# Two attention layers and two MLPs on one core: the value products of a key tile for all 512 queries in one group, behind the second pair's scores

## The chip, the cores and the metric

One core of one Trainium2 chip runs the whole kernel. The time is the device time of one execution in microseconds; the median of three executions is compared. The profile is of one further execution, taken by the hardware profiler. PE is the matrix engine (its weight loads are a row of their own, PEld), ACT the scalar engine, DVE the vector engine, POOL the general one, SP the engine that issues most DMAs. PE writes its results to PSUM, from where ACT and DVE read them.

## The reference

The input x has 2048 rows of 256 numbers, all in float32. Four layers follow each other:

```python
x = x + attn_a(layernorm(x))   # 16 query heads, 4 key/value heads, head size 16, rotary, biases
x = x + ffn(layernorm(x))      # 256 -> 2048 -> 256, gated tanh-gelu, 4-bit weights to be unpacked
x = x + attn_b(layernorm(x))   # 16 heads of 16, no rotary, no biases
x = x + ffn(layernorm(x))
```

Both attentions are causal over all 2048 positions:

```python
scores = einsum("bthd,bshd->bhts", q, k) * scale
scores = where(tril, scores, -inf)
attended = einsum("bhts,bshd->bthd", softmax(scores), v)
```

## The kernel before

The queries are cut into 4 blocks of 512 (b), the 16 heads into 4 groups of four (g). A unit is one (b, g): four heads and 512 queries against all keys up to the block's end, in 4(b+1) key tiles of 128. Each attention has 16 units, one after the other; `run` (L950) lists their steps, and `weave` (L43) puts the steps of one unit and side work into the one order in which every engine's queue is filled. The order is written by the program and kept: each engine takes its instructions in it.

A unit needs the row maxima first. They are found one unit ahead: `max_steps` (L752) multiplies queries by keys with queries on the partitions (L763, two heads at once in the two halves of the rows), and DVE reduces each result over the keys (L775). `gather` and `turn` bring the maxima into a form from which PE itself subtracts them.

`value_steps` (L824) does the unit proper. A key tile takes two steps, one for each pair of heads. `pair(kt, p)` (L852) writes a pair's scores with keys on the partitions: two small matmuls put the negative maxima in (L860), two add the scores (L865), and ACT takes the exponentials into a tile e in SBUF (L877). `values` (L829) then multiplies the exponentials of the key tile before by its values (L845): four matmuls, one a head, into four strips of 32 partitions of one PSUM tile ps_av, which is summed over all key tiles of the unit. A matmul of float32 numbers stands twice in the trace, so four matmuls are eight records. A column of ones beside the values gives the sums of the exponentials. `end` copies ps_av out, and `divide` turns it and divides. On the last four key tiles of a unit (the diagonal) only part of the queries is left: 512, 384, 256 and 128 of them, and triangular masks are added by further small matmuls (L738).

The scores of `pair` and of `max_steps` go to the same PSUM tiles: ps_s (L122) has three buffers of two banks each, used in turn. A buffer is free again when ACT has taken its exponentials, or DVE its maxima. The e tiles have four buffers, ps_av and ps_m one each.

In an ordinary place the order on PE is thus: scores of the first pair, a block of scores for the next unit's maxima, value products; scores of the second pair, another block for the maxima, value products. `values(0)` behind the first pair does the first 256 of 512 queries for all four heads, `values(1)` behind the second pair the other 256. A key tile with 256 queries or fewer is done whole behind the first pair; one with 384 in parts of 128 and 256. Only the last unit of each attention (b = 3, g = 3), which has no next unit and so no maxima beside it, does every key tile whole, behind the second pair. Beside the steps of a unit run further side steps: the projections of the next block of queries (`prep_steps`), the output projection of the block before (`out_steps`), and in the first attention the unpacking of the 4-bit weights.

`class Mlp` (L1018) then runs the feed-forward layer on the same ps_s, ps_m and ps_av buffers.

Of the kernel before, what the change touches and what calls it, by code (L numbers as in the profile page):

```python
# [27 lines left out]
NG = NH // 4  # L28
MLP = 2048
NFC = MLP // P  # L30
TB = 512
NB = S // TB
# [48 lines left out]
def tile_hybrid_layers(  # L81
# [40 lines left out]
    def ps_s():  # L122
        return psum.tile([P, 2, 512], F32, tag="s", name="ps_s", bufs=3)

    def ps_av():
        return psum.tile([P, 512], F32, tag="av", name="ps_av")

    def ps_m():
        return psum.tile([P, 512], F32, tag="m", name="ps_m")
# [281 lines left out]
    class Attention:  # L411
# [412 lines left out]
        def value_steps(self, b, g):  # L824

            nk = NT * (b + 1)
            held = {"pending": []}

            def values(half):  # L829


                self.settle()
                kt, q0, es_ = held["pending"][0]
                whole = (b, g) == (NB - 1, NG - 1)
                few = whole or TB - q0 <= TB // 2
                if half == 1:
                    held["pending"].pop(0)
                if few and half != whole:
                    return
                if kt == 0 and half == whole:  # L840
                    held["av"] = ps_av()
                own = slice(q0, TB) if few else slice(*((q0, TB // 2), (TB // 2, TB))[half])
                for j in range(4):
                    h = g if self.first else 4 * g + j
                    nc.tensor.matmul(  # L845
                        held["av"][32 * j : 32 * j + 32, own],
                        lhsT=self.vv[kt // NT][:, kt % NT, h * VW : h * VW + 32],
                        rhs=es_[j // 2][:, j % 2, own],
                        start=(kt == 0 and half == whole), stop=(kt == nk - 1),
                    )  # L850

            def pair(kt, p):  # L852
                q0 = max(0, kt - NT * b) * P
                diagonal = kt >= NT * b
                keys = slice((kt % NT) * P, (kt % NT + 1) * P)
                self.settle()
                pt = ps_s()

                for r in range(2):
                    nc.tensor.matmul(  # L860
                        pt[:, r, q0:], lhsT=sel[64 * r : 64 * r + 64, p, :],
                        rhs=self.mT[b, g][64 * r : 64 * r + 64, q0:], start=True, stop=False,
                    )
                for r in range(2):
                    nc.tensor.matmul(  # L865
                        pt[:, r, q0:], lhsT=self.key_rows(kt // NT, g, p, r, keys),
                        rhs=self.qT[b, g][64 * r : 64 * r + 64, p, q0:],
                        start=False, stop=not diagonal,
                    )
                e = self.wk.tile([P, 2, TB], F32, tag="e", name="e", bufs=4)  # L870

                def masked():
                    self.add_mask(pt, 1, q0)
                    exponentials()

                def exponentials():
                    nc.scalar.activation(e[:, :, q0:], pt[:, :, q0:], AF.Exp, scale=QK_SCALE)  # L877

                if diagonal:
                    self.owed.append(("exp", masked))  # L880
                else:
                    exponentials()
                if p == 0:
                    held["es"] = [e]
                else:
                    held["pending"].append((kt, q0, held["es"] + [e]))

            def end():
                values(0)
                values(1)  # L890
                o = pre.tile([P, TB], F32, tag="o", name="o")
                nc.scalar.copy(o, held["av"])
                held["o"] = o

            def divide():
                o = held["o"]
                pt = ps_m()
                for i in range(NT):
                    nc.tensor.transpose(
                        pt[:, i * P : (i + 1) * P], o[:, i * P : (i + 1) * P], ident  # L900
                    )
                heads = pt.rearrange("p (t j c) -> p t j c", t=NT, c=32)
                rec = small.tile([P, NT, 4], F32, tag="rec", name="rec")
                nc.vector.reciprocal(rec, heads[:, :, :, HD])
                if g == 0:
                    self.att[b] = pre.tile([P, NT, NG, 4, HD], F32, tag="att", name="att")
                nc.vector.tensor_tensor(
                    self.att[b][:, :, g], heads[:, :, :, :HD],
                    rec.unsqueeze(3).broadcast_to([P, NT, 4, HD]), ALU.mult,
                )  # L910

            steps = []
            for kt in range(nk):
                for p in range(2):
                    scored = lambda kt=kt, p=p: pair(kt, p)
                    steps.append((scored, lambda p=p: values(p)) if kt else scored)
            return steps, end, divide
# [295 lines left out]
```

## Time and profile before

| | |
|---|---|
| median of 3 runs | 1848.21 us (1847.87 to 1849.67) |
| the profiled execution | 1858.67 us |
| its span, first to last instruction | 1856.9 us |
| granted PE clock, mean | 0.987 |
| PE busy | 1775.3 us, 96% |
| DVE busy | 1127.8 us, 61% |
| ACT busy | 802.9 us, 43% |
| first attention, first pair of the first unit to first pair of the last | 46.9 to 583.4 us |
| second attention, the same | 976.2 to 1480.2 us |
| a unit of the last block (second attention, g = 1 and 2) | 46.4 and 46.3 us |

In the groups of the profile a row gives the line, the engine, the operation, the tile written and the tiles read, the shape and the count, then busy time, the mean of one in ns and the idle time ahead of it. In the timeline the first number is the start in us, the second the length; x8 is eight records that lie together, and a bracket gives the idle time of that engine just before and whose end closed it. PE's matmuls are pipelined and their ends are modelled, so the distance from one start to the next is what a group of matmuls really takes.

### The profile page before, as it was taken

The numbers are of one execution on the slowest core, as the hardware profiler recorded it, in microseconds if no ns is written. First come the engines' busy times: TensorE is split into PE (matmuls) and PEld (weight loads), VectorE is DVE, ScalarE is ACT, GpSimd is POOL, SyncE is SP. The second block draws the span as 40 slices with busy tenths as digits, with TensorE's granted clock in tenths as the row PEclk, the third lists the DMA queues.
The fourth block names the chain that finished last, engine by engine and source line by source line (L and its number), as shares of the span: only waits on it lengthen the run. The fifth ranks groups of instructions, "written<-read, shape, count | busy, mean of one in ns | idle before, by whom it ended". The sixth has DMA issues, their size and how long they took to land. (4 is left out here: it accounts for less than half of the span.)

```text
span 1856.9 us, 31581 instructions
## 1 busy us (share of the span) xinstructions
PE 1775.3 (96%) x13342; PEld 923.2 (50%) x13342; DVE 1127.8 (61%) x1679; ACT 802.9 (43%) x1071; POOL 240.2 (13%) x444
## 2 busy tenths in 40 slices
PE   9889989999999999999998998999999999999999
PEld 4444444444443465747464444444444434655656
DVE  4567778788785544363545677767877726354442
ACT  1335455556667422132314354565666663132221
POOL 4031201120012211012101010000000001011110
PEclk7799999999999999999999999999999999999999
DMA  5131300120000200003203314014000010000000
GB/s 137 49 75 44 74 31 24 32 61 19 24 13 30 91 6 1 1 1 74 51 0 77 62 49 79 13 46 72 22 12 2 1 46 1 12 3 9 7 6 12
DMA packets 41887, 63.43 MB, mean 34 GB/s; under 512 B 13713, under 2 KB 20753, under 8 KB 41489
## 3 DMA queue, kind: packets, MB, share of 16 engines
q1 hardware_dynamic: 33104, 45.41, 8.4%
q0 software_dynamic: 7680, 15.48, 5.0%
q8 instruction: 105, 1.72, 0.4%
q10 hardware_dynamic: 960, 0.52, 0.1%
q14 instruction: 38, 0.30, 0.1%
HBM read 43.45 MB, written 17.83 MB: 33 GB/s over the span
## 5 line engine op out<-in xcount | busy, mean ns | idle before, releaser
L775 DVE TENSOR_REDUCE mx<-ps_s 128x2 f32<-128x1024 f32 (+3 forms) x640 | 660.6, 1061 | 224.9 <-PE ps_s L738 114.9
L877 ACT ACTIVATE e<-ps_s 128x1024 f32<-128x1024 f32 (+3 forms) x640 | 568.8, 898 | 401.9 <-PE ps_s L865 229.7
L845 PE MATMUL ps_av<-e,v 128*32 128x256 f32 (+2 forms) x4384 | 351.5, 392 | 0.0
L865 PE MATMUL ps_s<-qT,kT 64*128 64x512 f32 (+3 forms) x1280 | 336.4, 523 | 0.0
L763 PE MATMUL ps_s<-kT,qT 64*128 64x512 f32 (+3 forms) x1280 | 269.7, 422 | 29.8 <-ACT e L877 13.5
L860 PE MATMUL ps_s<-mT,sel 64*128 64x512 bf16 (+3 forms) x1280 | 231.2, 355 | 25.0 <-ACT mT L817 10.7
L1062 PE MATMUL ps_s<-xnT,wg 128*128 128x512 f32 x512 | 240.9, 593 | 0.0
L1062 PE MATMUL ps_s<-xnT,wu 128*128 128x512 f32 x512 | 240.6, 592 | 0.0
L860 PEld LDWEIGHTS <-sel 64*128 64x128 bf16 x1280 | 75.1, 93 | 252.5 <-issue 243.1
L763 PEld LDWEIGHTS ps_s<-kT,qT 64*128 64x128 f32 x1280 | 129.0, 187 | 140.3 <-ACT e L877 65.3
L1068 ACT ACTIVATE t<-ps_s 128x512 f32<-128x512 f32 x128 | 76.3, 596 | 243.8 <-PE ps_s L1062 243.6
L1071 ACT ACTIVATE t<-t 128x512 f32<-128x512 f32 x128 | 80.5, 629 | 199.2 <-DVE t L1070 199.2
L1070 DVE TENSOR_TENSOR t<-ps_s,t 128x512 f32<-128x512 f32 x128 | 88.1, 689 | 123.5 <-POOL t L1069 121.5
L1062 PEld LDWEIGHTS ps_s<-xnT,wu 128*128 128x128 f32 x512 | 97.3, 190 | 122.5 <-issue 122.5
L1069 POOL TENSOR_SCALAR t<-t 128x512 f32<-128x512 f32 x128 | 79.4, 620 | 533.8 <-ACT t L1068 530.3
L1062 PEld LDWEIGHTS ps_s<-xnT,wg 128*128 128x128 f32 x512 | 95.1, 190 | 104.2 <-issue 102.5
L1072 DVE SCALAR_TENSOR_TENSOR t<-t,ps_s 128x512 f32<-128x512 f32 x128 | 88.2, 689 | 89.0 <-ACT t L1071 89.0
L845 PEld LDWEIGHTS ps_av<-e,v 128*32 128x32 f32 x4384 | 87.2, 108 | 94.3 <-issue 79.9
L865 PEld LDWEIGHTS ps_s<-qT,kT 64*128 64x128 f32 x1280 | 129.2, 197 | 0.0
L1087 PE MATMUL ps_m<-wd,inter 128*128 128x256 f32 x512 | 114.5, 380 | 0.0
L1087 PE MATMUL ps_av<-wd,inter 128*128 128x256 f32 x512 | 114.5, 380 | 0.0
L1087 PEld LDWEIGHTS ps_av<-wd,inter 128*128 128x128 f32 x512 | 96.7, 190 | 17.1 <-issue 4.5
(147 smaller groups left out, 1221.6 us busy)
## 6 DMA issues: line engine op xcount, KB each, us to landing
qT<-h SPq DMA_DIRECT2D x248, 64.0 KB, 2.2
kT<-h POOLq DMA_DIRECT2D x88, 128.0 KB, 5.4
h<-high SPq DMA_DIRECT2D x24, 256.0 KB, 2.1
h<-low SPq DMA_DIRECT2D x24, 256.0 KB, 2.2
wd<-wd_kept SPq DMA_DIRECT2D x2, 2048.0 KB, 7.8
wd_kept<-dq_d SPq DMA_DIRECT2D x4, 512.0 KB, 2.7
out<-x SPq DMA_DIRECT2D x16, 128.0 KB, 1.7
x<-x SPq DMA_DIRECT2D x3, 512.0 KB, 7.6
```

The source lines that it names most:

```text
L763: nc.tensor.matmul(pt[:, r, :w], lhsT=self.qT[b, g][64 * r : 64 * r + 64, p, i * P : (i + 1) * P], rhs=self.key_rows(c, g, p, r, slice(0, w)),
L775: nc.vector.tensor_reduce(held["mx"][:, i, 2 * p : 2 * p + 2, c], pt[:, :, :w], AX.X, ALU.max)
L845: nc.tensor.matmul(held["av"][32 * j : 32 * j + 32, own], lhsT=self.vv[kt // NT][:, kt % NT, h * VW : h * VW + 32], rhs=es_[j // 2][:, j % ...
L860: nc.tensor.matmul(pt[:, r, q0:], lhsT=sel[64 * r : 64 * r + 64, p, :], rhs=self.mT[b, g][64 * r : 64 * r + 64, q0:], start=True, stop=False,)
L865: nc.tensor.matmul(pt[:, r, q0:], lhsT=self.key_rows(kt // NT, g, p, r, keys), rhs=self.qT[b, g][64 * r : 64 * r + 64, p, q0:], start=Fals ...
L877: nc.scalar.activation(e[:, :, q0:], pt[:, :, q0:], AF.Exp, scale=QK_SCALE)
L1062: nc.tensor.matmul(pt[:, k, :], lhsT=w[:, c, fc * P : (fc + 1) * P], rhs=self.xnT[b][:, c, :], start=(c == 0), stop=(c == 1),)
L1069: nc.gpsimd.tensor_scalar(t, t, GELU_A, 1.0, ALU.mult, ALU.add)
L1070: nc.vector.tensor_tensor(t, gate, t, ALU.mult)
L1071: nc.scalar.activation(t, t, AF.Tanh, scale=GELU_C)
L1072: nc.vector.scalar_tensor_tensor(t, t, 1.0, gate, ALU.add, ALU.mult)
L1087: nc.tensor.matmul(po[:, :D], lhsT=inter[:, fc, i * P : (i + 1) * P], rhs=wd[:, fc, :], start=(fc == 0), stop=(fc == NFC - 1),)
```

## The change

The two halves of `values` become one. Behind the first pair of a key tile nothing is done but what is owed for the masks; behind the second pair the four matmuls are issued for all queries that are left of the key tile before, up to 512. The two special cases, the last unit and the tiles of 256 queries or fewer, fall away, since all units now follow one rule. The line numbers behind the change are four lower: L845 becomes L841, L860 L856, L865 L861, L877 L873.

```diff
             def values(half):
 
-
                 self.settle()
                 kt, q0, es_ = held["pending"][0]
-                whole = (b, g) == (NB - 1, NG - 1)
-                few = whole or TB - q0 <= TB // 2
-                if half == 1:
-                    held["pending"].pop(0)
-                if few and half != whole:
+                if half == 0:
                     return
-                if kt == 0 and half == whole:
+                held["pending"].pop(0)
+                if kt == 0:
                     held["av"] = ps_av()
-                own = slice(q0, TB) if few else slice(*((q0, TB // 2), (TB // 2, TB))[half])
+                own = slice(q0, TB)
                 for j in range(4):
                     h = g if self.first else 4 * g + j
                     nc.tensor.matmul(
                         held["av"][32 * j : 32 * j + 32, own],
                         lhsT=self.vv[kt // NT][:, kt % NT, h * VW : h * VW + 32],
                         rhs=es_[j // 2][:, j % 2, own],
-                        start=(kt == 0 and half == whole), stop=(kt == nk - 1),
+                        start=(kt == 0), stop=(kt == nk - 1),
                     )
```

## The prediction

> **What bounds the kernel now.** I read the page's engine shares first, then its costliest groups, then the waits, and last the timeline of single steps. I write S for the two mask and two score matmuls of one pair (L860, L865), M for one score block of the next unit's maxima (L763), V for a group of value products (L845). S and M each take one of three buffers of ps_s; ACT frees that of an S (exponential, L877), DVE that of an M (reduction, L775).
>
> ```profile
> PE 1775.3 (96%) x13342; PEld 923.2 (50%) x13342; DVE 1127.8 (61%) x1679; ACT 802.9 (43%) x1071; POOL 240.2 (13%) x444
> ...
> L845 PE MATMUL ps_av<-e,v 128*32 128x256 f32 (+2 forms) x4384 | 351.5, 392 | 0.0
> ```
>
> PE is busy nearly all the time, so what shortens PE's work shortens the kernel, as long as PE doesn't wait instead. Who makes it wait is in the waits:
>
> ```profile
> PEld ps_s L763 <- ACT e L877: 65.3, 178, 1.5
> PEld ps_s L763 <- DVE mx L775: 44.6, 113, 1.4
> ```
>
> M is what waits, mostly for ACT: for the buffer of an earlier S. One ordinary step of a late unit (second attention, third block of keys complete) shows how near this lies:
>
> ```profile
> 1395.48 0.39 PE L860 MATMUL ps_s<-mT,sel 64*128 64x512 bf16 x2
> ...
> 1396.20 1.02 ACT L877 ACTIVATE e<-ps_s 128x1024 f32<-128x1024 f32 x1 [0.48 <-PE ps_s L865]
> ...
> 1396.83 0.39 PE L860 MATMUL ps_s<-mT,sel 64*128 64x512 bf16 x2
> ...
> 1397.28 0.19 PEld L763 LDWEIGHTS ps_s<-kT,qT 64*128 64x128 f32 x2 [0.24 <-ACT e L877]
> 1397.29 0.49 PE L763 MATMUL ps_s<-kT,qT 64*128 64x512 f32 x2
> ...
> 1397.71 0.64 PE L845 MATMUL ps_av<-e,v 128*32 128x256 f32 x8
> 1398.28 0.39 PE L860 MATMUL ps_s<-mT,sel 64*128 64x512 bf16 x2
> ```
>
> From start to start: S 0.46, M 0.42, V 0.57, a step of 1.45 us, two of them for a key tile. The order is S M V S M V. With three buffers, the M at 1397.29 takes the buffer of the S at 1395.48, three uses back. That S's exponential starts 0.72 later, lasts 1.02 and ends at 1397.22; M starts 0.07 behind it. So an M follows the S three uses before it by at least 0.72 + 1.02 + 0.06 = 1.80 us. Today S, M, V, S lie between the two, 1.91 us of PE work: the wait is just covered, and V is what covers it.
>
> Where V is missing, the wait is open. At the start of a unit there is no key tile whose values could be taken yet:
>
> ```profile
> 1388.70 0.39 PE L860 MATMUL ps_s<-mT,sel 64*128 64x512 bf16 x2
> ...
> 1389.20 0.50 PE L763 MATMUL ps_s<-kT,qT 64*128 64x512 f32 x2
> ...
> 1389.72 0.39 PE L860 MATMUL ps_s<-mT,sel 64*128 64x512 bf16 x2
> ...
> 1390.60 0.19 PEld L763 LDWEIGHTS ps_s<-kT,qT 64*128 64x128 f32 x2 [0.67 <-ACT e L877]
> 1390.60 0.49 PE L763 MATMUL ps_s<-kT,qT 64*128 64x512 f32 x2 [0.25 <-ACT e L877]
> ```
>
> S M S M: the second M starts 0.88 us behind its S where 0.42 to 0.46 is usual, 1.90 behind the first S. (ACT was also held some 0.1 by the copy of o.) In the 22 units that start so, with two or more blocks of keys, this distance lies between 1.89 and 2.22.
>
> **What the change does, and its terms.** By the instruction order of the two kernels, 198 key tiles lose their two V of 256 queries for one of 512, behind the second M; 30 lose a V of 128 and one of 256 for one of 384. The last unit of each attention has this form already, and the narrower diagonal tiles only move by one step. No other engine's order changes.
>
> Term 1, the merged V. The last unit shows the form:
>
> ```profile
> 1493.05 0.10 PEld L860 LDWEIGHTS <-sel 64*128 64x128 bf16 x2 [0.26 <-issue]
> 1493.06 0.39 PE L860 MATMUL ps_s<-mT,sel 64*128 64x512 bf16 x2
> ...
> 1493.60 1.07 PE L845 MATMUL ps_av<-e,v 128*32 128x512 f32 x8
> 1494.60 0.39 PE L860 MATMUL ps_s<-mT,sel 64*128 64x512 bf16 x2
> ```
>
> 1.00 from V to the next S, against 2 x 0.57 = 1.14: 0.14 saved. The two V of 384 there take 0.78, against 0.57 + 0.36 = 0.93: 0.15 saved. In all 198 x 0.14 + 30 x 0.15 = 32 us less for PE. A rule would make this smaller: the Trainium skill, "TensorE: Matmul & The Clock Gate", Part 2, Back-to-back issue gap, puts a warm matmul at its columns over 2.4 GHz plus 2.5 ns. By that eight records fewer save 20 ns a key tile, 228 x 0.02 = 5 us. The rows show a fixed part of 0.14 for a group of eight records in four column strips (0.57 for 256 columns, 1.00 for 512), and I take the rows: 32.
>
> Term 2, the wait that V covered. The order becomes S M S M V. Start the first S at 0. M follows at 0.46, the second S at 0.87, and PE reaches the second M at 1.33. It needs the first S's buffer, which is free at 1.80: a stall of 0.47. V stands behind that M in PE's order, so it can't fill the gap, though its exponentials have long been there; behind V stand all later scores. Then M 0.34 (as short as it is after a wait) and V 1.00: the next S starts at 3.14. That S takes the first M's buffer: reduction from 0.46 + 0.54 = 1.00 to 2.23 (0.54 and 1.23 by the rows at 1390.60 and 1391.14 of the same timeline), so it has no wait. Period 3.14.
>
> I sorted the 198 periods (first S of a key tile to the first S of the next) of the trace by what lies in them:
>
> - 49 full-width with two M and nothing else: now 2.92 on average, then 3.14: +0.22, +10.8 us.
> - 51 full-width with three M. S M M S M V: the second S needs the first S's buffer, 1.80; the third M the first M's, 2.28; V at 2.62, next S at 3.62. S M S M M V ends at 3.6 too. Three reductions of 1.23 are 3.69. I take 3.65 against 3.42 now: +11.7 us.
> - 7 with four M: four reductions are 4.9 us, DVE sets them before (4.3 with narrow blocks among them) and after: 0.
> - 19 on the first diagonal tile without other work: the S of 384 queries, its masks and an exponential of 0.81 free the buffer at 1.95, and ten periods of 3.17 become 1.95 + 0.28 + 0.23 + 1.00 = 3.46; the other nine like them. About +0.25 each: +4.7 us.
> - 72 in which PE does something else too (projections, transposes, 0.6 to 2 us). In 53 it lies ahead of the fourth buffer use and covers the wait; 19 still have it, 10.4 us together. Against that, 72 x 0.14 = 10.1: 0.
> - the 30 tiles of 384: their pairs have few M beside them, no new wait: -4.5 us.
>
> Sum: 10.8 + 11.7 + 4.7 + 0 - 4.5 = +22.7 us. In other words, stalls of 82 us (the same count by distance alone, 145 tiles at 0.57), of which 27 take the place of waits that PE has today (2.92 and 3.42 are more than the bare work; DVE's backlog, too, is worked off in the stall), less 32.
>
> Moves at no price: the V of 256 queries on the third diagonal tile goes from behind the first S to behind the second; no M lies there, its exponentials are over, cost between 0 and 0.1 for 30 tiles, I take 0. The e buffers (four): V still ends before the S whose exponential reuses them, 0.72 ahead; no new wait. The accumulation stays in the one ps_av; its first V comes one step later, by which the copy of o of the unit before is long done. The gated clock: PE's new gaps are half a microsecond, like those that it has at each unit start, where the clock row stays at 9 of 10; 0.
>
> The profiled execution took 1858.67 us (span 1856.9 and 1.8 around it), 10.5 above the median of the runs, 1848.21. The sum is 1.2% of either: a profiled execution near 1881, a median of 1871.
>
> **Rivals.** (A) Slower by about 23 us, as above: chance 0.73, +8 to +42. For it: the wait can be read at every unit start, and PE's order is fixed.
> (B) Faster: the merged V pays and the buffer wait hardly adds. The skill speaks for it: "Perfetto Trace Analysis", Optimizing Tensor Performance, Matmuls, says "Larger matmuls are more efficient than smaller matmuls, when possible." By that alone the sum is term 1, -32 us, 1816. The trace agrees about the V and disagrees about its surroundings; the same section wants groups to rotate through banks so that evacuation overlaps, and three buffers are what runs out here. Mechanism: the new stalls merely replace PE waits of today. It decides where new stalls net of vanished ones come below 32 us, 0.22 a tile on 145 tiles; I find 82 - 27 = 55, 0.38 a tile. Chance 0.11, 1816 to 1844.
> (C) Nothing given back: all 82 us of stall stand, PE's other waits remain: 82 - 32 = +50, 1898. For it: at unit starts the stall comes on top of the rest. Chance 0.13.
> (D) The two terms cancel within 0.2% (3.7 us, about what measurement can tell from no change): 0.03.
>
> **How the numbers follow.** The likeliest is A, 1871. B is below 1848, C is near 1898; a range from 1855 to 1899 holds A and most of C, and leaves out B and D and a tail of C, less than 2 in 10. A alone gives 1856 to 1890. Faster 0.11, within 0.2% 0.04, slower 0.85.
>
> **What would show it.** Right: V groups of eight records at 1.00 from V to S; the wait of M's weight loads on ACT's e rising from 65 us to over 110; in late units a period of 3.1 to 3.2 with the second M about 0.8 to 0.9 behind its S, where now 0.42 is usual; units two and three of the last block (46 us) up by about 3 us. The MLP stretches and the last unit of each attention unchanged. Wrong: a second M that starts at its usual 0.42 behind S (an exponential that frees its buffer earlier than 1.80), or V costing other than 1.00 beside M; or DVE's waits shrinking so much that periods with three M don't grow.

## The result and the profile after

| | before | after |
|---|---|---|
| median | 1848.86 us (1847.87 to 1849.67, 4 runs) | 1880.95 us (1879.07 to 1883.33, 4 runs) |
| ratio | | 1.0165 (95%: 1.0136 to 1.0193) |
| profiled execution, span | 1858.67, 1856.9 us | 1880.94, 1879.2 us |

The change makes the kernel 32 us slower. In the profiles the two attentions take 15.2 and 13.7 us longer between the points that were measured before (40.2 to 591.9 and 984.7 to 1502.4 now), and what lies between and behind these stretches is the same. That the two profiled spans differ by 22 only has its reason ahead of them: in the profile before, the first pair starts at 46.9, in the profiles of all other kernels here between 38.4 and 42.8.

On the page of the kernel after, PE's shares and the group of the value products:

```profile
PE 1725.9 (92%) x11518; PEld 872.0 (46%) x11518; DVE 1128.8 (60%) x1679; ACT 794.7 (42%) x1071; POOL 239.9 (13%) x444
...
L841 PE MATMUL ps_av<-e,v 128*32 128x512 f32 (+3 forms) x2560 | 303.8, 546 | 0.0
```

PE has less to do, 1725.9 us in place of 1775.3, and the time grew all the same: what is new is idle PE. The waits name it (engine and line that wait, whom for, us in total, times, longest), first in the kernel before, then in the one after:

```profile
PE ps_s L763 <- ACT e L877: 13.5, 33, 1.3
PE ps_s L763 <- DVE mx L775: 12.6, 32, 1.0
...
PE ps_s L860 <- DVE mx L775: 4.9, 14, 0.7
PE ps_s L860 <- ACT e L877: 3.9, 13, 1.4
```

```profile
PEld ps_s L763 <- ACT e L873: 102.5, 141, 1.5
PE ps_s L763 <- ACT e L873: 48.4, 99, 1.3
PE ps_s L856 <- ACT e L873: 33.0, 52, 1.4
PE ps_s L856 <- DVE mx L775: 17.2, 34, 1.2
PE ps_s L763 <- DVE mx L775: 10.7, 23, 1.1
```

Weight loads of M waited 65.3 us for ACT before, 102.5 now. The four rows of PE itself add up to 109.3 us; before, they came to 34.9. That is 74 us of new waits for a buffer of ps_s. One plain key tile of the same unit as in the prediction, in the timeline of the kernel after:

```profile
1425.78 0.39 PE L856 MATMUL ps_s<-mT,sel 64*128 64x512 bf16 x2
...
1426.25 0.40 PE L763 MATMUL ps_s<-kT,qT 64*128 64x512 f32 x2
...
1426.49 0.39 PE L856 MATMUL ps_s<-mT,sel 64*128 64x512 bf16 x2
...
1426.51 1.94 ACT L873 ACTIVATE e<-ps_s 128x1024 f32<-128x1024 f32 x2 [1.29 <-PE ps_s L861]
...
1427.59 0.18 PEld L763 LDWEIGHTS ps_s<-kT,qT 64*128 64x128 f32 x2 [0.90 <-ACT e L873]
1427.59 0.50 PE L763 MATMUL ps_s<-kT,qT 64*128 64x512 f32 x2 [0.48 <-ACT e L873]
...
1428.01 1.07 PE L841 MATMUL ps_av<-e,v 128*32 128x512 f32 x8
...
1429.01 0.39 PE L856 MATMUL ps_s<-mT,sel 64*128 64x512 bf16 x2
```

S M S, then 0.48 us in which PE does nothing, M, V, and S again after 3.23. The second M follows the first S, three uses of a buffer back, by 1.81. (A float32 matmul of V stands twice in the rows, one of M or of the scores once: two matmuls, x2.) The two units of the last block of keys (second attention, g = 1 and 2) went from 46.4 and 46.3 to 49.9 and 49.7; the MLP stretches and the last units did not change (their full tiles last 2.22 on average in both traces).

### The profile page after: what moved, and what is told of

Its sections match the earlier page's. It is cut to its first block, busy times and chain, and to the rows that moved or that the text cites. A ratio compares the mean times of both kernels' runs of the same rounds, so it can differ in the third digit from the quotient of the medians.

```text
span 1879.2 us, 27933 instructions
## 1 busy us (share of the span) xinstructions
PE 1725.9 (92%) x11518; PEld 872.0 (46%) x11518; DVE 1128.8 (60%) x1679; ACT 794.7 (42%) x1071; POOL 239.9 (13%) x444
## 5 line engine op out<-in xcount | busy, mean ns | idle before, releaser
L873 ACT ACTIVATE e<-ps_s 128x1024 f32<-128x1024 f32 (+3 forms) x640 | 562.1, 898 | 447.4 <-PE ps_s L861 256.8
L861 PE MATMUL ps_s<-qT,kT 64*128 64x512 f32 (+3 forms) x1280 | 333.9, 522 | 0.0
L763 PE MATMUL ps_s<-kT,qT 64*128 64x512 f32 (+3 forms) x1280 | 261.4, 414 | 62.5 <-ACT e L873 48.4
L841 PE MATMUL ps_av<-e,v 128*32 128x512 f32 (+3 forms) x2560 | 303.8, 546 | 0.0
L856 PE MATMUL ps_s<-mT,sel 64*128 64x512 bf16 (+3 forms) x1280 | 230.5, 355 | 52.4 <-ACT e L873 33.0
L856 PEld LDWEIGHTS <-sel 64*128 64x128 bf16 x1280 | 73.1, 93 | 333.1 <-issue 326.9
L763 PEld LDWEIGHTS ps_s<-kT,qT 64*128 64x128 f32 x1280 | 124.2, 187 | 172.6 <-ACT e L873 102.5
L1058 PEld LDWEIGHTS ps_s<-xnT,wg 128*128 128x128 f32 x512 | 95.1, 190 | 104.2 <-issue 102.5
L861 PEld LDWEIGHTS ps_s<-qT,kT 64*128 64x128 f32 x1280 | 128.7, 196 | 0.0
L1083 PEld LDWEIGHTS ps_m<-wd,inter 128*128 128x128 f32 x512 | 96.9, 190 | 14.3 <-issue 1.1
```

Of the source, the lines that this page charges most:

```text
L763: nc.tensor.matmul(pt[:, r, :w], lhsT=self.qT[b, g][64 * r : 64 * r + 64, p, i * P : (i + 1) * P], rhs=self.key_rows(c, g, p, r, slice(0, w)),
L841: nc.tensor.matmul(held["av"][32 * j : 32 * j + 32, own], lhsT=self.vv[kt // NT][:, kt % NT, h * VW : h * VW + 32], rhs=es_[j // 2][:, j % ...
L856: nc.tensor.matmul(pt[:, r, q0:], lhsT=sel[64 * r : 64 * r + 64, p, :], rhs=self.mT[b, g][64 * r : 64 * r + 64, q0:], start=True, stop=False,)
L861: nc.tensor.matmul(pt[:, r, q0:], lhsT=self.key_rows(kt // NT, g, p, r, keys), rhs=self.qT[b, g][64 * r : 64 * r + 64, p, q0:], start=Fals ...
L1058: nc.tensor.matmul(pt[:, k, :], lhsT=w[:, c, fc * P : (fc + 1) * P], rhs=self.xnT[b][:, c, :], start=(c == 0), stop=(c == 1),)
L1083: nc.tensor.matmul(po[:, :D], lhsT=inter[:, fc, i * P : (i + 1) * P], rhs=wd[:, fc, :], start=(fc == 0), stop=(fc == NFC - 1),)
```

## The experiments

The theory. A buffer is held for H, from the start of the matmuls that fill it until its reader lets it go. A key tile S M S M uses a buffer four times, and there are three. So the fourth use waits until the first lets go, at least H after it started; then comes PE's own stretch from the fourth use to the next, which no hold hides. A key tile lasts at least H plus that stretch, and the longest stretch sets it: with M and V in it, 1.81 + (0.42 + 1.00) = 3.23. Twelve kernels, in the order of what they ask. Ratios are to runs of the kernel before on the same chip, with 95% intervals.

**Is it the merging?** Both halves behind the second pair, unmerged:

```diff
+                whole = (b, g) == (NB - 1, NG - 1) or TB - q0 <= TB // 2
+                owns = [slice(q0, TB)] if whole else [slice(q0, TB // 2), slice(TB // 2, TB)]
+                for n, own in enumerate(owns):
                     for j in range(4):
...
```

> The halves stay apart (two groups of 256 queries), but both stand behind the second pair's block of maxima, where the changed kernel has its one group. Buffer theory: a buffer of ps_s comes back 1.81 us after its S starts, so a key tile lasts at least 1.81 plus the longest stretch of PE between two uses of a buffer; that stretch is 0.42 + 2 x 0.57 = 1.56 here, so 3.37 us for a plain tile where the changed kernel has 3.23. All 228 merged tiles lose their 0.14: about 1881 + 32 = 1913 us. Rival, the merged form itself is what costs (512 columns at once slow PE or its neighbours): the halves would be as before, about 1849.

Measured: 1879.82 us, 1.0163 (1.0149 to 1.0177). Neither theory's number. It is the same as the kernel with merged V, tile for tile: plain tiles 3.25 on average in both. Its timeline:

```profile
1426.26 1.07 PE L843 MATMUL ps_av<-e,v 128*32 128x256 f32 x16
1427.27 0.39 PE L858 MATMUL ps_s<-mT,sel 64*128 64x512 bf16 x2
```

Sixteen records of 256 columns take 1.01 to the next S, as eight of 512 do. So the fixed 0.14 does not belong to a group of eight; it belongs to going into V and out of it. The merging saves nothing that shows; having one stretch of V in a key tile instead of two saves the 0.14. The whole loss, too, comes from where V stands.

**Is V merely stuck behind a waiting M?** V ahead of the second M, and V behind the first:

```diff
-                    steps.append((scored, lambda p=p: values(p)) if kt else scored)
+                    if kt and p and (b, g) != (NB - 1, NG - 1):
+                        steps.append(lambda scored=scored: (scored(), values(1)))
+                    else:
+                        steps.append((scored, lambda p=p: values(p)) if kt else scored)
...
```

> The whole V directly behind the second pair's scores and ahead of the second block of maxima (and of side work). Buffer theory: the longest stretch is now S and V, 0.46 + 1.00, and what it shortens is the time DVE has for a block of maxima (0.54 + 1.23 + 0.06 = 1.83): a plain tile lasts 1.83 + 1.46 = 3.29, no better than the changed kernel's 3.23; 1881 to 1895 us. Rival, V is merely stuck behind a waiting M in PE's order: in front of it V fills the gap, a plain tile takes its bare work, 2.75, and the kernel goes below the one before: 1816 to 1830.

```diff
-                kt, q0, es_ = held["pending"][0]
-                if half == 0:
+                if half != ((b, g) == (NB - 1, NG - 1)):
                     return
-                held["pending"].pop(0)
+                kt, q0, es_ = held["pending"].pop(0)
```

> The whole V behind the first pair's block of maxima instead of the second's. Buffer theory: the same longest stretch (M and V, 1.42) in another place, so the same 3.23 for a plain tile and the same time, 1873 to 1888 us. Rival, stuck behind the second M: 1816 to 1830.

Measured: 1906.91 us, 1.0309 (1.0295 to 1.0323), and 1897.70 us, 1.0259 (1.0243 to 1.0274). Both lie above their range, on the far side from the rival: no place of a whole V that was tried helps. In the timeline of the second of the two, V behind the first M:

```profile
1442.69 0.39 PE L855 MATMUL ps_s<-mT,sel 64*128 64x512 bf16 x2
...
1443.39 0.39 PE L855 MATMUL ps_s<-mT,sel 64*128 64x512 bf16 x2
...
1444.49 0.49 PE L763 MATMUL ps_s<-kT,qT 64*128 64x512 f32 x2 [0.48 <-ACT e L872]
1444.92 1.07 PE L840 MATMUL ps_av<-e,v 128*32 128x512 f32 x8
1445.92 0.39 PE L855 MATMUL ps_s<-mT,sel 64*128 64x512 bf16 x2
```

Again 3.23 and again 0.48 of idle PE. Counted from the second S on, all 26 tiles of the order S M S M V last 3.22 or 3.23. With V between the second S and its M the reader that comes late is DVE:

```profile
1442.70 0.50 PE L763 MATMUL ps_s<-kT,qT 64*128 64x512 f32 x2
...
1444.52 0.39 PE L856 MATMUL ps_s<-mT,sel 64*128 64x512 bf16 x2 [0.63 <-DVE mx L775]
```

An S waits for the M three uses back, 1.82 behind it; with S and V in one stretch (0.55 + 1.00) that makes 3.37. Counted in the same way, 25 of the 26 tiles S V M S M last 3.36 to 3.39.

So the plain tiles came as the theory says, and the totals did not. What they have more than the changed kernel stands in the last two key tiles of the units, those in which S has 256 and 128 queries. Measured from the kernel before, these tiles fell by 12.5 us in sum in the changed kernel; with V ahead of the second M they rose by 13.5, with V behind the first by 20.7. In the first of these two runs, PE waits longer for DVE before it turns the maxima (L811, 26.6 us against 13.1 in the changed kernel), which is about half of the difference. For the second the cause stays open.

**Is it the hold, then?** An exponential over half the queries shortens ACT's hold to about 1.38. The other half is left out; V reads the same half twice, so that PE's work stays. With the whole V and, as its control, with the halves:

```diff
-                    nc.scalar.activation(e[:, :, q0:], pt[:, :, q0:], AF.Exp, scale=QK_SCALE)
+                    own = slice(q0, (q0 + TB) // 2)
+                    nc.scalar.activation(e[:, :, own], pt[:, :, own], AF.Exp, scale=QK_SCALE)
...
```

> The changed kernel with an exponential of only half of each pair's queries; the value products read that half twice, so that PE's work stays the same (half of the exponentials are left out, the output is not the reference's). Buffer theory: ACT takes 0.60 instead of 1.02, the buffer comes back after 1.39, and a plain tile needs 1.39 + 1.42 = 2.81, about PE's own work (2.75): 1810 to 1830 us, 20 to 32 below its own control with halves. Rival, the new place of V costs PE by itself (order, switching between shapes): no change from 1881, and 25 to 35 above its control.

> The control: the kernel before with the same half exponentials. Buffer theory: its wait was just covered, so it gains little, 1838 to 1849 us. Rival: the same; the two are told apart by the difference to the run with the whole V.

Measured: 1833.17 us, 0.9916 (0.9902 to 0.9930), and the control 1814.90 us, 0.9819 (0.9804 to 0.9834). The whole V lost 48 us of its time, more than its excess; but its control lost 33 too, where I had expected ten at most, and stays 18 below it. By kinds of tile: full ones with two M are at 2.90 against the control's 2.83, those with three at 3.59 against 3.31. Three reductions of 1.23 are 3.69, so DVE was the next to hold buffers. Maxima over half of each block, with both forms, and with the whole V and full exponentials:

```diff
-                        held["mx"][:, i, 2 * p : 2 * p + 2, c], pt[:, :, :w], AX.X, ALU.max
+                        held["mx"][:, i, 2 * p : 2 * p + 2, c], pt[:, :, : w // 2], AX.X, ALU.max
...
```

> The changed kernel with half exponentials, as before, and also with maxima over only half of each block's keys (both left out by half, and the scale inside the exponential is a sixteenth, so that nothing overflows; the output is not the reference's). With half exponentials alone the whole V stayed 18 us above the halves; in its trace plain tiles came to 2.92, but tiles with three blocks of maxima stayed at 3.67 to 3.68, three reductions of 1.23. If DVE's hold on the buffers is the second part of the wait, it goes now: both buffers come back after 1.2 to 1.4, every tile takes PE's bare work, and the whole V gains its 0.14: 15 to 30 us below the control with halves, about 1775 to 1795. If something else made up those 18 us, this kernel stays above its control.

> The control: the kernel before with the same half exponentials and half maxima. Both theories: about 1800 to 1812, a little under the 1815 with half exponentials alone.

> The changed kernel with half maxima alone (left out as above; exponentials over all queries). If ACT's buffer is the one that comes last in the changed kernel, plain tiles stay at 3.23 to 3.27 and those with three blocks near 3.6: 1868 to 1880. If DVE's were the one, the time falls below 1850.

Measured: 1762.90 us, 0.9534 (0.9521 to 0.9547); 1754.14 us, 0.9486 (0.9471 to 0.9500); 1826.49 us, 0.9878 (0.9864 to 0.9891). The last one was to tell which reader comes last. Its plain tiles stay at 3.24 on average, as ACT's hold says, but elsewhere DVE's share was larger than I gave it: the whole kernel fell by 54 us, far below my 1868. Tiles with three M went to 3.47, where I had 3.6, and three of the eight units of the first block fell by 3 to 5 us each. Of the pair, the whole V still is 9 above its control, where I had it 15 to 30 below. Its plain tiles last 2.81, against the control's 2.71, and those with three M 3.15 against 2.94. For the plain tile no other cost is needed: it is the half exponential's own hold, 0.72 + 0.60 + 0.06, plus 1.42: 2.80. I had taken 2.75 for PE's bare work in the order S M S M V, and it is less: 0.46 + 0.24 + 0.46 + 0.42 + 1.00 = 2.58, since an S straight behind an M starts 0.24 after it. So the hold had to be cut once more, to a quarter of the exponentials:

> As the whole V with half exponentials and half maxima (1763), but exponentials over a quarter of the queries, read four times by the value products (three quarters of them are left out). In that run plain tiles last 2.79 to 2.81, which is again hold plus longest stretch: 0.72 + 0.60 + 0.06 + 1.42 = 2.80, and its control with halves is PE's bare work, 2.69. With a hold of 0.72 + 0.38 + 0.06 = 1.16 a plain tile can come to 2.58, which is also the bare work of the order S M S M V (0.46 + 0.24 + 0.46 + 0.42 + 1.00). Buffer theory: 1735 to 1750, now below the control with halves (1754). If the whole V behind the second pair costs PE something by itself, it stays at 1760 or above.

Measured: 1737.42 us, 0.9388 (0.9372 to 0.9403), 17 below the control with halves. A plain tile of this kernel:

```profile
1327.93 0.39 PE L857 MATMUL ps_s<-mT,sel 64*128 64x512 bf16 x2
...
1328.39 0.40 PE L763 MATMUL ps_s<-kT,qT 64*128 64x512 f32 x2
1328.63 0.39 PE L857 MATMUL ps_s<-mT,sel 64*128 64x512 bf16 x2
...
1329.09 0.50 PE L763 MATMUL ps_s<-kT,qT 64*128 64x512 f32 x2
...
1329.52 1.07 PE L841 MATMUL ps_av<-e,v 128*32 128x512 f32 x8
1330.52 0.39 PE L857 MATMUL ps_s<-mT,sel 64*128 64x512 bf16 x2
```

2.59, without a wait of PE. Plain tiles with the whole V thus last 3.25, 2.92, 2.81 and 2.60 on average, as holds go (full; half exponentials; half of both; a quarter and half). With the last, the hold plus 1.42 is below the 2.71 of the halves, and the whole V pays in a plain tile, by 0.1.

The 17 us as a whole are not that gain. By the periods of the two traces, full-width tiles with two M are 4.5 us below the control in sum, those with three M 6.4 above it (3.07 against 2.94). The 72 tiles with other work are 9.4 below, the last two key tiles of the units 15.7. PE's waits show one part of the latter, in the control:

```profile
PE ps_s L861 <- ACT mT L817: 10.7, 31, 0.7
PE ps_s L763 <- ACT e L879: 4.8, 12, 0.8
PE ps_m L811 <- DVE m_pad L798: 4.7, 2, 3.9
...
PE ps_s L861 <- ACT e L879: 1.2, 1, 1.2
```

In the kernel with the whole V the first row has 1.3 us, the third 7.3; the account of the last two diagonal tiles below says why. And the control's exponentials are halves, not quarters: that quarters would not bring it down as far is argued from its 6 us of waits for exponentials; it was not run.

**Where does it pay in the real kernel?** From the kernel before, V whole and behind the second pair in a part of the tiles: only the diagonal ones; only those with side work of PE in their first step; the diagonal ones and a choice among the others.

```diff
-                few = whole or TB - q0 <= TB // 2
+                few = whole = whole or q0 > 0
```

> From the kernel before: only the diagonal tiles with 384, 256 and 128 queries are done whole behind the second pair; tiles of 512 keep their two halves. By the prediction's terms 30 x 0.15 = 4.5 us less and no new wait: about 1844. If the later V of these tiles holds up what follows, 1849 to 1855.

```diff
+                if half == 0:
+                    held["covered"] = taken[0] > held["taken"]
+                whole = whole or (not few and held["covered"])
+                few = few or whole
...
```

> From the kernel before: a key tile's V is merged, and put behind the second pair, only where side work of PE stands between the two pairs' scores (49 tiles of 512, 7 of 384); elsewhere the halves stay. Buffer theory: that side work is longer than the stall of 0.5, so only the saving is left, 49 x 0.14 + 7 x 0.15 = 8 us less: about 1841. If a merged V costs in every surrounding, about 0.25 a tile more: about 1863.

Measured: 1848.39 us, 0.9996 (0.9988 to 1.0004), and 1848.38 us, 0.9998 (0.9989 to 1.0006): no difference in either. In the trace of the first, one wait goes and another comes: the first scores of a unit wait 1.3 us for the copy of the maxima (mT) where it was 10.7, the turn ahead of that copy waits 16.2 us for DVE where it was 7.6. In the trace of the second, twelve tiles with one piece of side work and three M fell as forecast, from 4.39 to 4.25; five with a piece in both steps rose from 5.83 to 6.26, and others of that kind too. One of these:

```profile
1047.87 0.66 PE L908 MATMUL ps_m<-ident,o 128*128 128x128 f32 x4
...
1048.92 0.39 PE L766 MATMUL ps_s<-kT,qT 64*128 64x512 f32 x2
...
1049.41 0.42 DVE L916 TENSOR_TENSOR att<-ps_m,rec 128x256 f32<-128x256 f32 x1
...
1049.98 0.63 PE L936 MATMUL ps_m<-ident,att 128*128 128x128 f32 x4 [0.68 <-DVE att L916]
```

Side work has one buffer, ps_m. The second piece waits until DVE has read the first; before, V and the work of another step lay between, and from M to that piece took 0.49 where it takes 1.06 now. It is the same rule at another buffer. Leaving those tiles out:

```diff
+                whole = whole or q0 > 0 or kt in ALONE.get((self.first, b, g), ())
+                few = whole
...
```

> From the kernel before: the diagonal tiles whole (as in the run with those alone), and 21 tiles of 512 whole, chosen from the last trace: those in which one piece of side work stands between the two pairs' scores and none behind. In that trace such tiles fell by 0.14 to 0.25, while tiles with side work in both steps rose by 0.4. If the rise is a wait for ps_m, the one buffer of all side work, which the V in between used to cover, leaving those tiles out leaves 21 x 0.15 = 3 us and 1 to 3 from the diagonal: 1843 to 1846, 0.15 to 0.3% below the kernel before. If the rise was chance, no difference from it.

Measured: 1842.84 us, 0.9967 (0.9954 to 0.9979), 6 us below the kernel before. That is the version that beats both kernels. It was meant to gain 3 to 6 and gained 6; the list ALONE names 21 tiles, all picked from the trace of the run above.

## Why the prediction was right, and which terms were off

It said slower, 1871 in a range of 1855 to 1899; it was 1880.95, +32 where the sum said +23. The mechanism held: M waits for ACT, the wait stands where V covered it, and V can't fill it. That the profiled execution came to the 1881 that was named for it is luck: the profiled execution before had lost 4 to 8 us ahead of its first pair. And the sum is closer than its terms, since some errors cancel. By the prediction's own classes, sums over the periods of the two traces:

| periods | forecast, us | measured, us |
|---|---|---|
| 49 full-width, two M | +10.8 | +17.2 (2.92 to 3.27) |
| 51 full-width, three M | +11.7 | +12.0 (3.42 to 3.66) |
| 7 full-width, four M | 0 | +2.4 |
| 19 first diagonal tile, nothing else | +4.7 | +3.9 |
| 72 with other work of PE, full-width or first diagonal | 0 | +6.8 |
| the last two diagonal tiles of 30 units, 60 periods | -4.5 | -12.5 |
| sum | +22.7 | +29.8 |

- Term 2, the plain tile: 3.14 was forecast, 3.22 to 3.25 came. The hold was right (1.80 against 1.81). Mis-sized was the M behind a wait: I took 0.34 until V, and it is 0.42 (1427.59 to 1428.01). 0.34 is what M takes where its weights were loaded ahead of it (the median of 76 such M in the trace before); here they are loaded only as it starts. 49 x 0.08 = 4 us of the 6 that are missing.
- Two of the signs named came out beside their numbers. The waits of M's weight loads for ACT rose to 102.5 us, not over 110; and the second M stands 1.10 behind its S, not 0.8 to 0.9, since an S straight behind an M that doesn't wait starts 0.24 after it (1426.25 to 1426.49), where I took 0.41.
- The 72 tiles with other work: "In 53 it lies ahead of the fourth buffer use and covers the wait", and I wrote 0. They cost 6.8. I had counted the uses of ps_s alone; the side work has its own buffer, ps_m, whose reading V also covered. The run with covered tiles and the one with chosen tiles show that.
- The last two diagonal tiles: -12.5 for -4.5. "Moves at no price" put at nothing what the move of V in the tile of 256 queries does. PE turns the next unit's maxima just ahead of the last pair's scores, ACT copies them, and the next unit's first S needs the copy. That V stood ahead of the turn; now it stands behind the last scores and covers the copy, while the turn waits longer for DVE. Before, then after:

```profile
PE ps_s L860 <- ACT mT L817: 10.7, 31, 0.7
PE ps_m L811 <- DVE m_pad L798: 7.6, 9, 3.4
```

```profile
PE ps_m L811 <- DVE m_pad L798: 13.1, 13, 3.8
...
PE ps_s L856 <- ACT mT L817: 1.3, 2, 0.7
```

That is 9.4 us less and 5.5 more, 4 of the 8 us. The rest stays open; the run with those tiles alone has the same order there, and its periods fell by 2.4 only.

- Term 1: 0.14 a tile is right in size and was put down to the wrong thing. I took it for a fixed part of each group and set the Trainium skill's rule aside ("TensorE: Matmul & The Clock Gate", Part 2, Back-to-back issue gap: 2.5 ns for each matmul, by which I estimated 20 ns a tile). The halves back to back take 1.01 against 1.00. For the merging as such the rule was nearer; the rest is the change from V to S, once a tile instead of twice.
- Rival B rested on the Trainium skill's "Larger matmuls are more efficient than smaller matmuls" ("Perfetto Trace Analysis", Optimizing Tensor Performance, Matmuls). No run here shows that for the merging: two groups back to back did as well as one large one. What pays in a plain tile once the holds are cut is one stretch of V in place of two. Rival C, at +50, would have needed PE's other waits to stay. The 74 us of new waits less the 32 saved would be +42; the time grew by 32, and the traces don't tell which waits went.

## What to carry to other kernels

Where results rotate through n buffers, work that doesn't use them is cover for the readers: look at what stands between one use and the use n later, and move nothing out of there before the hold is paid. Where a round has n + 1 uses, as here, it lasts at least the hold plus the longest stretch between two uses, so one long stretch can be worse than two short ones, even if it is less work in all. Another place for the long stretch changes only whose hold counts (plain tiles of 3.23, 3.23 and 3.37), but whole kernels differ (1881, 1898 and 1907). The moved work may have covered other waits where it stood, and may cover new ones where it goes. Count this for every buffer, the rarely used ones too: here ps_m lost its cover, and the copy of the maxima gained one.

## What the runs showed of the hardware that I had not expected

- Two groups of value products back to back cost PE as much as one of double width (1.01 and 1.00 us); two groups apart take 2 x 0.57, so going into V and out of it costs about 0.14.
- DVE's reductions hold the kernel more than its 61% suggests: with maxima over half the keys, the kernel with the whole V fell from 1880.95 to 1826.49, though its plain tiles didn't move.
- With half the exponentials the kernel with halves fell by 33 us (0.9819), though ACT is busy 43% of the time. I had called its wait "just covered", and even in the plain tile it was not quite: the hold plus M and half a V, 1.81 + 0.42 + 0.57 = 2.80, is above the 2.71 that these tiles last with both holds halved, and 2.79 is the shortest of the 31 in the kernel before (2.89 on average).
